# Layer 2's attention loop: sums and Newton step in other slots, values made four steps at a time

## The chip, the core and the metric

The kernel runs as one program on one core of a Trainium2 chip. The metric is device time in microseconds from start to end. The engines that matter here are TensorE (PE in the profile; its weight loads are PEld), VectorE (DVE), ScalarE (ACT), GpSimd (POOL) and the DMA queues. Each engine works through its own list of instructions in program order and waits on semaphores where it needs another's result. Matmul results go to PSUM[...].

## What is computed

The model is a chain of four cross-attention layers, each followed by a feed-forward layer, over 1024 tokens of width 128 and a context of 6404 rows. The change lies in the attention of layer 2. With 16 heads of width 8 its core is:

```python
qh = _split_heads(q @ Wq.T)
kh = _split_heads(k @ Wk.T)
vh = _split_heads(v @ Wv.T)
scores = jnp.einsum('bhqd,bhkd->bhqk', qh, kh) / jnp.sqrt(jnp.asarray(D, dtype=qh.dtype))
attn = jax.nn.softmax(scores, axis=1)
heads = jnp.einsum('bhqk,bhkd->bhqd', attn, vh)
return _merge_heads(heads) @ Wo.T
```

`q` is the normalized token matrix, `k` and `v` are both the context. The softmax runs over axis 1, the heads: for each pair of a token and a key, the 16 exponentials are divided by their own sum. So no sum over keys is needed, but every 128x512 block of scores needs a reciprocal of its own.

## The kernel before

`attn_heads` (L1268) works in steps. A step is one chunk of 128 keys (the 51st has 4) against one half of the tokens (512 columns): 51 chunks times two halves are 102 steps. A step has K = 8 slots; a slot handles two heads, so its tiles are [128 keys, 2 heads, 512 tokens]. From L1391 on the order of instructions on PE, ACT, DVE and POOL is the order written in the code (`manual_schedule`). One loop over slots (L1522 to L1549) writes it, with the parts of a step staggered over later slots. "Slot 0" to "slot 7" below mean the loop's `k`. In each slot it calls:

- `least_made` (L1348), ten slots ahead: two bf16 matmuls give approximate scores in the PSUM tile `pair_ps`, which has a single buffer; ScalarE copies them to `lb`. `least_so_far` (L1366), one slot later, folds them on VectorE into a running minimum (L1371; none in slot 7), and at a step's last pair into `mneg` (L1376). The minimum over heads keeps the exponentials in range.
- `exps` (L1431): four matmuls put the exact scores less the minimum into `x_ps` (two buffers), and ScalarE writes exponentials into `e` (L1445).
- `first_summed` (L1447), one slot later: a matmul with the identity adds one head into `s_ps` (one buffer), eight heads per step: those of pairs 0 to 3. So the first of a step, which stands in slot 1, writes into the buffer of the step before.
- `summed` (L1458), one slot later: VectorE adds pairs 4 to 7 with three additions of 128x1024 in slots 6, 7 and 0; also in slot 0 it adds the two halves of the result (L1470) and `s_ps` to it (L1471).
- `inverted` (L1475), in slot 1: the reciprocal of the sum, as Exp(-Ln) on ScalarE (L1480, L1481) and one Newton step on VectorE (L1482, L1483).
- `shared` (L1485), ten slots after `exps`: VectorE multiplies the pair by the reciprocal.
- `values` (L1492), thirteen slots after `exps`: matmuls of `e` with the values in `vz` collect in `o_ps`.
- `make_values` (L1417), once a step, in slot 5 and right ahead of the step's first `values`: a matmul (L1421) gives the values of 128 keys in `pair_ps`, and VectorE writes them, negated, into `vz` (L1425), in a layout with gaps: each head's 8 columns at the start of a 32-column group.

On PE the order in a slot is `least_made`, `exps`, `first_summed`, (`make_values`,) `values`. On VectorE it is (vz,) the minimum, the sums, the Newton step, the multiply. During the first steps the loop also makes the queries of the second half (`other`), and from step 55 on, in even slots, it takes pieces of the following feed-forward layer (`along`) until these are used up.

Of the kernel before, what the change touches and what calls it, by code (L numbers as in the profile page):

```python
# [10 lines left out]
F32 = mybir.dt.float32  # L11
# [4 lines left out]
AF = mybir.ActivationFunctionType  # L16
ALU = mybir.AluOpType
# [3 lines left out]
P = 128  # L21
S = 1024
NT = S // P
HALF = 512
HT = NT // 2
D = 128
# [18 lines left out]
class Net:  # L45
# [1222 lines left out]
    def attn_heads(self, ctxT, tiles, before, along):  # L1268
# [13 lines left out]
        nc, tc, a = self.nc, self.tc, self.a  # L1282
# [4 lines left out]
        K = NH // 2  # L1287
        scale = 8.0**-0.5
        with ExitStack() as st:
            kb, _, kst = tiles  # L1290
            big = st.enter_context(tc.tile_pool(name="a2big", bufs=1))
            qn = big.tile([P, 4, S], BF16, name="qn")
            qS = big.tile([P, 4, S], F32R, name="qS2")
            vz = [big.tile([P, 4 * 136], F32, name=f"vz{i}") for i in range(2)]
            wq = big.tile([P, D], F32, name="wq")
            wqs = big.tile([P, 4, D], F32, name="wqs")
            wv = big.tile([P, D], F32, name="wv")
# [42 lines left out]
            steps = [(c, at, n, half) for half in range(2) for c, (at, n) in enumerate(keys)]  # L1340
            N = len(steps)
            lows, mnegs, es, accs, sums, firsts, invs, kts, outs = ({} for _ in range(9))
# [5 lines left out]
            def least_made(slot):  # L1348

                i, k = divmod(slot, K)  # L1350
                c, at, n, half = steps[i]
                m = self.pair_tile()
                for t, (j, r) in enumerate(heads(k)):
                    nc.tensor.matmul(  # L1354
                        m[:n, t], kb[r, at : at + n], qn[r, j, ts(half, HALF)],
                        start=True, stop=True,
                    )
                if k == 0:
                    lows[i] = lp.tile([P, 2, HALF], BF16, tag="low", name="low")
                    t = lows[i]  # L1360
                else:
                    t = lp.tile([P, 2, HALF], BF16, tag="lb", name="lb", bufs=3)
                nc.scalar.copy(t[:n], m[:n])  # L1363
                return t
# [21 lines left out]
            pr = self.pool(st, "a2p", 2)  # L1386
# [11 lines left out]
            def exp_and_ln():  # L1398

                tc.keep_in_program_order(  # L1400
                    nc.scalar.preload_act_table_set("natural_log_exp_and_others")
                )

            def load_keys(i):
                _, at, n, _ = steps[i]
                kts[i] = pr.tile([P, 4, P], F32R, tag="kS", name="kS", bufs=3)
                if n < P:
                    nc.gpsimd.memset(kts[i].bitcast(F32), 0.0)
                for g in range(4):
                    nc.sync.dma_start(  # L1410
                        out=kts[i][32 * g : 32 * g + 32, :, :n].bitcast(F32),
                        in_=kst[P * g : P * g + P, at : at + n].rearrange(
                            "(j r) n -> r j n", j=4
                        ),
                    )

            def make_values(i):  # L1417

                _, at, n, _ = steps[i]
                m = self.pair_tile()  # L1420
                nc.tensor.matmul(m[:n, 0, :D], ctxT[:, at : at + n], wv, start=True, stop=True)  # L1421
                dst = vz[i % 2].rearrange("p (j x) -> p j x", x=136)[:n, :, :P]
                dst = dst.rearrange("p j (g y) -> p j g y", y=32)[:, :, :, :8]
                src = m[:n, 0, :D].rearrange("p (g j d) -> p j g d", g=4, j=4)
                nc.vector.tensor_scalar_mul(dst, src, -1.0)  # L1425

            def pair(i, k):
                at = 2 * (k % 2)
                return es[i, k // 2][: steps[i][2], at : at + 2]
# [16 lines left out]

            def first_summed(slot):  # L1447

                i, h = divmod(slot, K)
                if h == 0:  # L1450
                    firsts[i] = ps_s.tile([P, HALF], F32, tag="s", name="s_ps")
                n = steps[i][2]
                nc.tensor.matmul(  # L1453
                    firsts[i], self.ident[:n], es[i, h // 4][:n, h % 4],
                    start=h == 0, stop=h == K - 1,
                )

            def summed(slot):  # L1458
                i, k = divmod(slot, K)
                n = steps[i][2]  # L1460
                if k <= K // 2:
                    return
                if k == K // 2 + 1:
                    accs[i] = pr.tile([P, 2, HALF], F32, tag="acc", name="acc")
                acc = accs[i][:n]
                before = pair(i, k - 1) if k == K // 2 + 1 else acc
                nc.vector.tensor_tensor(acc, before, pair(i, k), ALU.add)
                if k == K - 1:
                    sums[i] = pr.tile([P, HALF], F32, tag="sum", name="sum")
                    nc.vector.tensor_tensor(sums[i][:n], acc[:, 0], acc[:, 1], ALU.add)  # L1470
                    nc.vector.tensor_tensor(  # L1471
                        sums[i][:n], firsts.pop(i)[:n], sums[i][:n], ALU.add
                    )

            def inverted(i):  # L1475

                n = steps[i][2]
                invs[i] = pr.tile([P, HALF], F32, tag="inv", name="inv")
                r, t, s = invs[i][:n], accs[i][:n, 0], sums[i][:n]
                nc.scalar.activation(t, s, AF.Ln)  # L1480
                nc.scalar.activation(r, t, AF.Exp, scale=-1.0)  # L1481
                nc.vector.tensor_tensor(t, s, r, ALU.mult)  # L1482
                nc.vector.scalar_tensor_tensor(r, t, 2.0, r, ALU.subtract, ALU.mult)  # L1483

# [7 lines left out]
            def values(i, j, part):  # L1492
                c, at, n, half = steps[i]
                if c == 0 and j == 0 and part == 0:
                    outs[half] = ps_o.tile([P, HALF], F32, tag="o", name="o_ps")
                for g in range(4):
                    cols = ts(part, HALF // 2)
                    nc.tensor.matmul(  # L1498
                        outs[half][32 * g : 32 * g + 32, cols],
                        vz[i % 2][:n, ds(P * j + 32 * g, 32)], es[i, j][:n, g, cols],  # L1500
                        start=c == 0 and j == 0 and part == 0,
                        stop=c == NK - 1 and j == 3 and part == 1,
                    )
                if c == NK - 1 and j == 3 and part == 1:
                    ob = lp.tile([P, HALF], F32, tag="q32", name="ob")
                    nc.scalar.copy(ob, outs[half])
                    y = self.m_tile()
                    for t in range(4):
                        nc.tensor.matmul(
                            y[:, ts(t, P)], ob[:, ts(t, P)], wo, start=True, stop=True  # L1510
                        )
                    self.add_to_tokens(y, half)

            SHARED = K + 2
            VALUES = K + 5
            SLOTS = N * K
            kept = {}
            other = make_queries(1)
# [3 lines left out]
            for slot in range(SLOTS + 3 * K):  # L1522
                i, k = divmod(slot, K)
                if k == 0 and i + 2 < N:
                    load_keys(i + 2)
                if slot + AHEAD < SLOTS:
                    kept[slot + AHEAD] = least_made(slot + AHEAD)
                if slot < SLOTS:
                    exps(slot)
                if 0 < slot <= SLOTS:  # L1530
                    first_summed(slot - 1)
                at = slot - VALUES
                if 0 <= at < SLOTS:
                    if at % K == 0:
                        make_values(at // K)
                    values(at // K, at % K // 2, at % 2)
                if slot - 1 + AHEAD in kept:
                    least_so_far(slot - 1 + AHEAD, kept.pop(slot - 1 + AHEAD))
                if 0 < slot <= SLOTS:
                    summed(slot - 1)  # L1540
                if 1 <= i <= N and k == 1:
                    inverted(i - 1)
                if 0 <= slot - SHARED < SLOTS:
                    shared(slot - SHARED)
                if 2 <= i < NK:
                    next(other, None)
                elif i >= NK + 4 and k % 2 == 0:
                    if next(along, None) == "other table":
                        exp_and_ln()  # L1549
# [414 lines left out]
```

## Time and profile before

| | us |
|---|---|
| median of 3 runs | 8147.5 (8136.12 to 8156.23) |
| the profiled execution: time | 8165.55 |
| the profiled execution: span of its instructions | 8163.5 |
| first to last start of L1445, layer 2's exponentials | 4231.0 to 6661.1 |

The granted TensorE clock is 0.959 of full speed over the whole span. Busy over the span are PE 7372.9 us (90%), DVE 6268.6 (77%) and ACT 4939.0 (61%).

Within layer 2's loop, by stretches of time (busy us of each engine, and the mean granted clock):

| stretch, us | what it holds | PE | DVE | ACT | clock |
|---|---|---|---|---|---|
| 4271 to 5377, 1105.5 us | steps of the first half | 995.8 | 972.4 | 811.4 | 0.99 |
| 5377 to 5464, 87.1 us | the chunk of 4 keys, change of halves | 80.1 | 61.3 | 51.2 | 0.78 |
| 5464 to 5534, 70.8 us | undisturbed | 62.0 | 63.8 | 50.0 | 1.00 |
| 5534 to 5885, 350.7 us | with pieces of the feed-forward layer | 297.7 | 316.9 | 233.0 | 0.94 |
| 5885 to 6622, 736.5 us | undisturbed | 669.9 | 643.0 | 537.5 | 0.97 |

How the lines in the next part are read. In the view of waits: who waited, for what, then the total in us, the number of times, and the longest. In the timeline: start in us, duration, engine, line, operation, out<-in, shapes, count, and in brackets the engine's idle time before it and what ended that. In the view of windows: the stretch, its length, the busy us of PE, PEld, DVE, ACT and POOL (instructions in brackets), the granted clock, the share of the DMA engines and GB/s. Consecutive VectorE operations overlap a little, so their starts lie closer than their durations: 1.13 to 1.14 us apart for 128x1024 fp32 (duration 1.22), 0.60 for the minimum (0.69).

### The profile page before, as it was taken

The page shows a single profiled execution, that of the slowest core. Times are in us where ns is not written, and L with a number is a line of the kernel's source. Part 1 is how long each engine was busy: PE and PEld are TensorE (multiplying, and loading weights), DVE is VectorE, ACT ScalarE, POOL GpSimd, SP SyncE. Part 2 cuts the span into 40 slices and gives each one's busy share as a digit, 9 for nine tenths or more (in the row PEclk, how much of TensorE's full clock was granted, in tenths as well). Part 3 has the DMA queues.
Part 4 walks back from the last instruction along what each step waited for, and adds up shares of the span by engine and source line. Part 5 has one row for each costly group of instructions (what it writes and reads, how often), then busy time and mean ns, then how long its engine had stood idle before and what let it go on. Part 6 is the DMA issues. An engine that isn't in the chain of part 4 may idle for free. (4 is left out here: it accounts for less than half of the span.)

```text
span 8163.5 us, 105249 instructions
## 1 busy us (share of the span) xinstructions
PE 7372.9 (90%) x41959; PEld 2806.6 (34%) x42169; DVE 6268.6 (77%) x7114; ACT 4939.0 (61%) x5829; POOL 1783.4 (22%) x1112
## 2 busy tenths in 40 slices
PE   6999999999999889999978999998899987999997
PEld 2333333333333433333343333332333323333334
DVE  6776777777775588888548888879888878888864
ACT  2444444444444467777757777766677746777765
POOL 4555555555556410000100000000000010000001
PEclk8999999999999899999989999999999978999988
DMA  1000000000000211010310000000000011100101
GB/s 29 1 2 2 1 2 1 2 2 1 1 1 1 73 28 16 11 19 11 112 37 11 12 12 13 12 10 11 11 12 12 12 45 32 19 11 13 17 5 39
DMA packets 145602, 134.96 MB, mean 17 GB/s; under 512 B 31530, under 2 KB 126054, under 8 KB 144206
## 3 DMA queue, kind: packets, MB, share of 16 engines
q1 hardware_dynamic: 134214, 104.37, 5.8%
q0 software_dynamic: 5936, 18.04, 0.7%
q8 instruction: 331, 5.42, 0.3%
q10 hardware_dynamic: 4960, 5.80, 0.2%
q14 instruction: 161, 1.32, 0.1%
HBM read 105.46 MB, written 35.85 MB: 17 GB/s over the span
## 5 line engine op out<-in xcount | busy, mean ns | idle before, releaser
L897 DVE TENSOR_REDUCE mx<-pair_ps 128x2 f32<-128x1024 f32 x1612 | 1811.3, 1178 | 253.8 <-PE pair_ps L893 229.8
L285 DVE TENSOR_REDUCE mx<-b_ps 128x2 f32<-128x1024 f32 x920 | 1091.5, 1186 | 639.5 <-PE b_ps L281 636.9
L331 ACT ACTIVATE pt<-x_ps,bias 128x1024 f32<-128x1024 f32 (+1 forms) x944 | 1000.9, 1110 | 877.6 <-PE x_ps L326 844.5
L345 POOL TENSOR_TENSOR acc<-acc,pt 128x1024 f32<-128x1024 f32 x544 | 1341.9, 2467 | 537.0 <-ACT pt L331 524.6
L1126 ACT ACTIVATE px<-x_ps 128x1024 f32<-128x1024 f32 x1088 | 1113.8, 1024 | 308.9 <-PE x_ps L1121 301.7
L1363 ACT CAST lb<-pair_ps 128x1024 bf16<-128x1024 f32 (+1 forms) x714 | 722.1, 1012 | 507.0 <-PE pair_ps L1354 494.6
L1453 PE MATMUL s_ps<-e,ident 128*128 128x512 f32 (+1 forms) x1632 | 877.7, 620 | 136.2 <-DVE sum L1471 134.8
L1490 DVE TENSOR_TENSOR e<-e,inv 128x1024 f32<-128x1024 f32 (+1 forms) x816 | 993.4, 1218 | 0.0
L351 PE MATMUL o_ps<-pt,v 128*64 128x512 f32 (+1 forms) x3776 | 915.9, 605 | 0.0
L1012 PE MATMUL o_ps<-px,v 128*32 128x512 f32 x4352 | 904.1, 620 | 0.0
L1012 PE MATMUL o_ps<-py,v 128*32 128x512 f32 x2176 | 896.7, 616 | 0.0
L326 PE MATMUL x_ps<-q,kT 64*128 64x512 f32 (+1 forms) x3776 | 894.8, 592 | 0.0
L893 PE MATMUL pair_ps<-kb,qz 64*128 64x512 bf16 (+1 forms) x3224 | 827.8, 386 | 59.8 <-DVE mx L897 33.7
L1445 ACT ACTIVATE e<-x_ps 128x1024 f32<-128x1024 f32 (+1 forms) x816 | 841.0, 1031 | 34.6 <-PE x_ps L1442 34.6
L1126 ACT ACTIVATE py<-y_ps 128x512 f32<-128x512 f32 x1088 | 647.7, 595 | 323.8 <-PE y_ps L1121 322.9
L1121 PE MATMUL x_ps<-qS,kS 33*128 33x512 f32 x2176 | 711.7, 531 | 127.9 <-ACT px L1126 127.9
L345 DVE TENSOR_TENSOR acc<-acc,pt 128x1024 f32<-128x1024 f32 (+1 forms) x368 | 629.6, 1711 | 66.2 <-ACT pt L331 66.1
L1498 PE MATMUL o_ps<-e,vz 128*32 128x256 f32 (+1 forms) x6528 | 546.6, 407 | 57.3 <-DVE vz L1425 53.2
L1121 PE MATMUL y_ps<-qS,kS 33*128 33x512 f32 x1088 | 567.4, 522 | 4.3 <-ACT py L1126 4.3
L1371 DVE TENSOR_TENSOR low<-lb,low 128x1024 bf16<-128x1024 bf16 (+1 forms) x714 | 488.4, 684 | 8.7 <-ACT lb L1363 8.5
L1438 PE MATMUL x_ps<-qS,kS 32*128 32x512 f32 x1632 | 487.8, 593 | 0.0
L1442 PE MATMUL x_ps<-mneg,identb 128*128 128x512 bf16 x1422 | 454.9, 390 | 34.5 <-issue 34.5
(374 smaller groups left out, 8010.2 us busy)
## 6 DMA issues: line engine op xcount, KB each, us to landing
kS<-kst SPq DMA_DIRECT2D x400, 64.0 KB
kS<-kd SPq DMA_DIRECT2D x112, 200.1 KB
w<-in_L_ffn_w SPq DMA_DIRECT2D x48, 256.0 KB
kst<-kd POOLq DMA_DIRECT2D x24, 512.0 KB, 13.7
kd<-kh SPq DMA_DIRECT2D x12, 512.0 KB
kd<-k SPq DMA_DIRECT2D x12, 512.0 KB
qS<-qd SPq DMA_DIRECT2D x256, 16.0 KB
kb<-in_L_ffn_w SPq DMA_DIRECT2D x16, 256.0 KB
```

Source lines behind the costliest of these rows:

```text
L285: nc.vector.tensor_reduce(mxs[u][:, t, :, b], m[:, :, :n], AX.X, ALU.max)
L326: nc.tensor.matmul(s[:n, g], kT[p % 2][r, at : at + n], qs[p][r, ts(half, HALF)], start=False, stop=True,)
L331: nc.scalar.activation(pt[:n], s[:n], AF.Exp, bias=bias[:n, c : c + 1])
L345: eng.tensor_tensor(acc[:n], acc[:n], pt[:n], ALU.add)
L351: nc.tensor.matmul(o[cols], v[:n, c, cols], pt[:n, g], start=c == 0, stop=c == NKT - 1)
L897: nc.vector.tensor_reduce(mxs[u][:, t, b], m[:, :, :n], AX.X, ALU.max)
L1012: nc.tensor.matmul(o[32 * j : 32 * j + 32], v[:, c, ds(VW * h, 32)], pt, start=i == 0, stop=c + 2 >= NK,)
L1121: nc.tensor.matmul(s[:, k], kS[p % 2][r, ts(c, P)], qS[u % 2][r], start=True, stop=True,)
L1126: nc.scalar.activation(pt[:, : len(some)], s[:, : len(some)], AF.Exp)
L1445: nc.scalar.activation(pair(i, k), s[:n], AF.Exp)
L1453: nc.tensor.matmul(firsts[i], self.ident[:n], es[i, h // 4][:n, h % 4], start=h == 0, stop=h == K - 1,)
L1490: nc.vector.tensor_tensor(e, e, r, ALU.mult)
```

## The change

`make_values` now makes the values of four steps with four matmuls into one half of a pair tile, and ScalarE copies them, negated, into a new buffer `v4` with one activation (or one per step where a chunk is short). A new `spread_values`, once a step, lays out one step's part of `v4` into `vz` on ScalarE. `first_summed` takes heads 0 to 5 and 10, 11 (pairs 0, 1, 2 and 5); VectorE adds pairs 3, 4, 6 and 7, in slots 5, 7 and 0, and the two 128x512 additions come in slot 1 of the next step. `inverted` keeps Ln and Exp, now in slot 2; the Newton step becomes `improved`, in slot 3. The multiply comes eleven slots after `exps` instead of ten, the value matmuls fourteen instead of thirteen. `spread_values` is called two slots ahead of a step's first value matmul, in slot 4; `make_values` five slots ahead, in slot 1 of every fourth step, behind the value matmuls of its slot on PE.

```diff
+            v4 = big.tile([P, 4, D], F32, name="v4")
...
             def make_values(i):
...
-                _, at, n, _ = steps[i]
-                m = self.pair_tile()
-                nc.tensor.matmul(m[:n, 0, :D], ctxT[:, at : at + n], wv, start=True, stop=True)
+                four = steps[i : i + 4]
+                m = self.pair_tile()[:, 0].rearrange("p (s d) -> p s d", d=D)
+                for s, (_, at, n, _) in enumerate(four):
+                    nc.tensor.matmul(
+                        m[:n, s], ctxT[:, at : at + n], wv, start=True, stop=True
+                    )
+                full = [n == P for _, _, n, _ in four]
+                if all(full):
+                    nc.scalar.activation(v4[:, : len(four)], m[:, : len(four)], AF.Copy, scale=-1.0)
+                    return
+                for s, (_, at, n, _) in enumerate(four):
+                    nc.scalar.activation(v4[:n, s], m[:n, s], AF.Copy, scale=-1.0)
+
+            def spread_values(i):
+                n = steps[i][2]
                 dst = vz[i % 2].rearrange("p (j x) -> p j x", x=136)[:n, :, :P]
                 dst = dst.rearrange("p j (g y) -> p j g y", y=32)[:, :, :, :8]
-                src = m[:n, 0, :D].rearrange("p (g j d) -> p j g d", g=4, j=4)
-                nc.vector.tensor_scalar_mul(dst, src, -1.0)
+                nc.scalar.copy(dst, v4[:n, i % 4].rearrange("p (g j d) -> p j g d", g=4, j=4))
...
             def first_summed(slot):
...
-                i, h = divmod(slot, K)
-                if h == 0:
+                i, k = divmod(slot, K)
+                if k == 0:
                     firsts[i] = ps_s.tile([P, HALF], F32, tag="s", name="s_ps")
                 n = steps[i][2]
+                h = k if k < 6 else k + 4
...
             def summed(slot):
+
                 i, k = divmod(slot, K)
+                if k == 0:
+                    i -= 1
+                if i < 0:
+                    return
                 n = steps[i][2]
-                if k <= K // 2:
-                    return
-                if k == K // 2 + 1:
+                if k == 4:
                     accs[i] = pr.tile([P, 2, HALF], F32, tag="acc", name="acc")
-                acc = accs[i][:n]
-                before = pair(i, k - 1) if k == K // 2 + 1 else acc
-                nc.vector.tensor_tensor(acc, before, pair(i, k), ALU.add)
-                if k == K - 1:
-                    sums[i] = pr.tile([P, HALF], F32, tag="sum", name="sum")
+                    nc.vector.tensor_tensor(accs[i][:n], pair(i, 3), pair(i, 4), ALU.add)
+                elif k in (6, 7):
+                    acc = accs[i][:n]
+                    nc.vector.tensor_tensor(acc, acc, pair(i, k), ALU.add)
+                elif k == 0:
+                    acc = accs[i][:n]
+                    sums[i] = pr.tile([P, HALF], F32, tag="sum", name="sum", bufs=1)
                     nc.vector.tensor_tensor(sums[i][:n], acc[:, 0], acc[:, 1], ALU.add)
...
                 nc.scalar.activation(t, s, AF.Ln)
                 nc.scalar.activation(r, t, AF.Exp, scale=-1.0)
+
+            def improved(i):
+                n = steps[i][2]
+                r, t, s = invs[i][:n], accs[i][:n, 0], sums[i][:n]
                 nc.vector.tensor_tensor(t, s, r, ALU.mult)
                 nc.vector.scalar_tensor_tensor(r, t, 2.0, r, ALU.subtract, ALU.mult)
...
-            SHARED = K + 2
-            VALUES = K + 5
+            SHARED = K + 3
+            VALUES = K + 6
...
                 if 0 <= at < SLOTS:
-                    if at % K == 0:
-                        make_values(at // K)
                     values(at // K, at % K // 2, at % 2)
+                if 0 <= at + 2 < SLOTS and (at + 2) % K == 0:
+                    spread_values((at + 2) // K)
+                if 0 <= at + 5 < SLOTS and (at + 5) % (4 * K) == 0:
+                    make_values((at + 5) // K)
...
-                if 0 < slot <= SLOTS:
+                if 0 < slot <= SLOTS + 1:
                     summed(slot - 1)
-                if 1 <= i <= N and k == 1:
+                if 1 <= i <= N and k == 2:
                     inverted(i - 1)
+                if 1 <= i <= N and k == 3:
+                    improved(i - 1)
```

More of the change, by code (lines that the diff above doesn't have):

```diff
@@ L1447, in first_summed @@
             def first_summed(slot):
-                i, h = divmod(slot, K)
-                if h == 0:
+                i, k = divmod(slot, K)
+                if k == 0:
                     firsts[i] = ps_s.tile([P, HALF], F32, tag="s", name="s_ps")
                 n = steps[i][2]
+                h = k if k < 6 else k + 4
                 nc.tensor.matmul(
                     firsts[i], self.ident[:n], es[i, h // 4][:n, h % 4],
-                    start=h == 0, stop=h == K - 1,
+                    start=k == 0, stop=k == K - 1,
                 )
```

## The prediction

> **What bounds the kernel now.** The change touches one stage, so I first asked the page where that stage lies: the exponentials of L1445 run from 4231.0 to 6661.1 us and the value matmuls of L1498 end at 6681, about 2.45 ms of a span of 8163.5. In the busy times of that stretch PE (TensorE) stands at about 90% and DVE (VectorE) at 87%: shares that do not say which of them sets the pace. The starts of the value matmul L1421, one per step, do: among the undisturbed steps 22.46 us is by far the commonest distance.
>
> Next, who waits for whom from 4350 to 5370 us, 45 steps without other work:
>
> ```profile
> DVE vz L1425 <- PE pair_ps L1421: 106.6, 45, 3.7
> PEld s_ps L1453 <- ACT e L1445: 86.1, 44, 2.2
> PE s_ps L1453 <- DVE sum L1471: 66.3, 45, 1.8
> ```
>
> PE waits for VectorE once a step (1.47 us on average), and VectorE for PE once a step (2.4 us). Each holds the other up: a loop, not one full engine. The timeline around the first wait, at full clock:
>
> ```profile
> 5066.23 0.39 PE L1354 MATMUL pair_ps<-qn,kb 32*128 32x512 bf16 x2
> ...
> 5067.17 0.69 DVE L1470 TENSOR_TENSOR sum<-acc 128x512 f32<-128x512 f32 x1
> ...
> 5067.96 0.69 DVE L1471 TENSOR_TENSOR sum<-s_ps,sum 128x512 f32<-128x512 f32 x1
> ...
> 5068.80 1.10 PE L1453 MATMUL s_ps<-e,ident 128*128 128x512 f32 x2 [1.41 <-DVE sum L1471]
> ...
> 5070.40 0.39 PE L1354 MATMUL pair_ps<-qn,kb 32*128 32x512 bf16 x2
> ...
> 5071.39 1.02 PE L1453 MATMUL s_ps<-e,ident 128*128 128x512 f32 x2
> ...
> 5072.92 0.39 PE L1354 MATMUL pair_ps<-qn,kb 32*128 32x512 bf16 x2
> ```
>
> The reader is to see that a slot without a wait takes PE 2.52 us (5070.40 to 5072.92), its sum matmul starting 0.99 after the slot does, and that this one takes 4.17: s_ps has one buffer, and the first sum matmul of a step needs L1471 of the step before. The other wait, in VectorE's timeline one step earlier and later:
>
> ```profile
> 5057.77 0.29 DVE L1425 TENSOR_SCALAR vz<-pair_ps 128x128 f32<-128x128 f32 x1 [2.17 <-PE pair_ps L1421]
> ...
> 5080.23 0.29 DVE L1425 TENSOR_SCALAR vz<-pair_ps 128x128 f32<-128x128 f32 x1 [2.16 <-PE pair_ps L1421]
> ```
>
> Now the loop closes. From the end of L1471 (5068.65): 0.15 to PE's restart, 1.60 to the next slot, three slots 7.56, 2.27 to the vz copy, and from a vz copy to the next end of L1471 10.88 (5057.77 to 5068.65). Sum **22.46**, the measured step. In PE's ledger: 8 x 2.52 = 20.16, 0.67 at the values (such a slot takes 3.19) and 1.63 at the sum.
>
> The clock matters too. After the longer idle at 5021 the granted clock (third column from the right) falls to half:
>
> ```profile
> 5022.00:5023.00 1.00, 0.64 (x2) 0.30 (x2) 1.00 (x2) 0.72 (x2) 0.00 (x0) 0.93 0.03 8
> 5023.00:5024.00 1.00, 1.00 (x6) 0.17 (x8) 1.00 (x3) 0.54 (x1) 0.00 (x0) 0.50 0.00 0
> 5026.00:5027.00 1.00, 0.79 (x3) 0.42 (x2) 1.00 (x3) 0.84 (x2) 0.00 (x0) 0.86 0.00 0
> ```
>
> It lasts some 3.4 us and makes the step 24.03 instead of 22.46, so 1.57 dearer. Of 68 undisturbed steps with a gap of 1.40, 13 show it; of 11 with a gap of 1.75 (a pause of VectorE of 0.46 ahead of L1471, every fourth step of the first half), 5.
>
> **The change, part by part.** *The vz copy leaves VectorE* (102 x 0.29 = 30 us). Its own time is hidden; what goes is its wait, and with it PE's 0.67 per step, 68 us in all. ScalarE gets 102 strided 128x128 copies: no row shows the form; the nearest are 372 ns (a 128x128 activation, L635) and 249 ns (a 4x128 copy, L268). I take 0.37, 38 us if nothing hid it, in slot 4, where ScalarE idles 0.58 before the next lb. The Trainium skill (ScalarE: Activation LUTs, Rules for kernel authors) speaks against it: multiplies belong on VectorE. By that rule the move loses 0.08 per step; by the row it takes away a wait of 2.16. Neither 0.29 nor 0.37 is on the path, so the row of the wait decides.
>
> *Values of four steps at once.* 26 blocks. Four matmuls of the same shape take 1.16 (L1509 at 5459.89), 0.04 to ScalarE, 0.60 for its 128x512 copy (597 ns, L1324), 0.05 to the matmul of the next slot that needs the single pair buffer: 1.85, some 0.05 of it under the matmuls before: **1.8**. Behind that pair matmul waits all of PE. Bounds: 1.4, if weight loads hide and the matmuls run in 0.8; 2.7 at half clock, where the four take 2.07. The block stands in slot 1, right after the stalled sum, so it lies on the loop: 26 x 1.8 = 47 us, 0.45 per step.
>
> *Which pairs the two engines sum* (0, 1, 2 and 5 on PE; 3, 4, 6 and 7 on VectorE): counts equal, no cost.
>
> *The sums move from slot 0 to slot 1, the Newton step to slot 3, Ln and Exp to slot 2.* This decides. L1471 now stands in the very slot whose sum matmul waits for it, where before it stood one slot ahead; and Newton can begin only when ScalarE has done slot 2's exponential, Ln and Exp. Round the new loop, from the end of the sum: 0.15 and 1.60 to PE's slot 2; 1.34 to its exponential (5070.40 to 5071.74); 0.94 to Ln (1.03 less the usual overlap); 0.66 to Exp (5068.69 to 5069.35); 0.66 to Newton (5716.58 to 5717.24): 5.35. Then VectorE until the next sum ends, no wait on the way: two Newton operations, each waiting for its forerunner, 2 x 0.72 = 1.44; nine 128x1024 operations (six multiplies, three adds) at their spacing of 1.135, 10.22; five minima at 0.60, 3.00; mneg 0.12 + 0.34; L1470 to L1471 0.79; L1471 0.69: 16.60. Loop **21.95**. VectorE's idle moves to before Newton: its two multiplies and two minima after the sum end at 3.39, Newton comes at 5.35, so it waits 1.96 there instead of 2.16 before vz. Queued behind Newton are the multiplies that the value matmuls need, but three slots ahead of use. Ln and Exp in slot 2 make ScalarE 0.6 late in slot 3; its 0.48 of slack per slot absorbs that.
>
> PE's wait does not go: slot 1 begins at 1.75 + 7 x 2.52 = 19.39 and restarts at 22.10, 2.71 later against 2.57 before. The gap grows from 1.41 to 1.55.
>
> **Sum.** Three steps of 21.95 and one of 23.75: mean 22.40 against 22.46, -0.06 x 102 = **-6 us**. Falls of the clock: 19% at 1.40 and 45% at 1.75 give about 30% at 1.55; 79 undisturbed steps x 0.30 = 24 against 18, 6 x 1.57 = **+9 us**. Here the skill's rule (TensorE: Matmul & The Clock Gate, HAM oscillation) is that idle gaps above about 3.4 us re-throttle; by it neither kernel falls and the sum is -6; by the rows it is +3. I follow the rows. The 13 steps that carry the next layer's quantization (5534 to 5885, 27.0 each, VectorE busy 24.4): its operations come at the end of even slots. Before, those of slots 0, 2 and 4 lay between the sum and the vz copy, where VectorE waited; in the new loop only slot 2's fall into a wait. About 4.3 per step are added (24.4 less 20.1 in quiet steps); three quarters of it on the new loop make 21.95 + 3.2 = 25.2, 0.8 above VectorE's own total: 13 x 0.8 = 10 us lost at worst, against 0.67 per step won at the values, 9. I take 0, within 10.
>
> Together +3 us. On the profiled run (8165.55 us, span 8163.5, 18 above the median of the three runs) that is 8169; on the median 8147.5, **8150**.
>
> **Rivals.**
> - *No measurable change, as summed*: 0.52. Own range 8125 to 8172.
> - *Slower: a clock fall with every block.* PE idles 1.55 at the sum, works 2.7, then idles 0.65 for ScalarE's copy. If each of some 20 undisturbed blocks brings a fall besides 30% of the other 59 steps, that is 38 falls, 14 more than I count: +22; if the matmuls then run at half clock, a block costs 2.7 instead of 1.8: 20 x 0.9 = +18. 8150 + 40 = 8190. It decides once about 14 falls come on top. For it: falls grow with the gap; against: the second gap alone is below any that a fall followed. 0.31.
> - *Faster: the wait at the sum shrinks to nothing*, PE's 20.16 + 0.45 = 20.6 per step; 1.8 x 79 = 142 us: 8005. It is what dealing the sums evenly would give if VectorE could run ahead (its 20.0 per step would fit); against it stands the loop, which needs no full engine. 0.05. A milder form: a step of 22.40 whose rhythm avoids falls saves 6 + 18 x 1.57 = 34: 8114. 0.12.
>
> The change does what it says: the sums are dealt; only the wait they feed is not.
>
> **Numbers.** About 0.3% (24 us) is what a measurement of this kernel can tell from no change. Faster 0.05 + 0.12 = 0.17; within 0.52; slower 0.31. The range 8105 to 8205 takes in the milder gain and the slower rival with its dearer blocks and leaves out the large gain.
>
> **What would show it.** In the new trace: no wait before a vz write; VectorE idle about 2 us before the Newton multiply in each step; PE still idle 1.5 to 1.6 at the first sum matmul; distances between those of 21.95, 21.95, 21.95 and 23.75 at full clock; the clock at half after about 24 of the undisturbed steps. Wrong it would be if PE's gap at the sum were under 1 us (the loop does not hold), if a block cost above 2.3, or if half clock followed most steps.

## The result, and the profile after

The changed kernel takes 8188.2 us (median of four runs, 8180.6 to 8195.6) against 8142.1 (8136.1 to 8156.2), four runs as well. The recorded ratio, which is not the quotient of the two medians, is 1.0051, with an interval of 1.0038 to 1.0063. It is 46 us slower, inside the stated range, but not the "no measurable change" held likeliest, whose own range ended at 8172. The profiled execution has a span of 8178.9 us.

The undisturbed steps did what the sum said. Here is the view of waits of the changed kernel over the same stretch as before, 4350 to 5370 us (who waited, for what, total us, times, longest; a selection):

```profile
PE s_ps L1466 <- DVE sum L1489: 68.3, 44, 1.6
DVE acc L1504 <- ACT inv L1499: 64.5, 45, 1.7
ACT v L1428 <- PE pair_ps L1423: 40.4, 11, 4.7
PE pair_ps L1355 <- ACT v L1428: 7.5, 11, 0.7
```

The wait before vz is gone. PE's wait at the sum is not (1.55 us each time), and VectorE's wait now stands before the Newton step. The timeline of one such step, slots 1 to 3, shows both:

```profile
5122.77 0.39 PE L1355 MATMUL pair_ps<-qn,kb 32*128 32x512 bf16 x2
...
5124.65 0.69 DVE L1489 TENSOR_TENSOR sum<-s_ps,sum 128x512 f32<-128x512 f32 x1
...
5125.49 1.10 PE L1466 MATMUL s_ps<-e,ident 128*128 128x512 f32 x2 [1.56 <-DVE sum L1489]
...
5127.09 0.39 PE L1355 MATMUL pair_ps<-qn,kb 32*128 32x512 bf16 x2
...
5128.56 0.69 DVE L1372 TENSOR_TENSOR low<-lb,low 128x1024 bf16<-128x1024 bf16 x1 [0.35 <-ACT lb L1364]
...
5130.66 0.69 DVE L1504 TENSOR_TENSOR acc<-sum,inv 128x512 f32<-128x512 f32 x1 [1.41 <-ACT inv L1499]
```

PE starts its slot 1 at 5122.77, and its sum matmul 2.72 later, because L1489 ends only at 5125.34. VectorE idles 0.35 and 1.41 before Newton. Some distances between steps (starts of mneg, L1376 before and L1377 after, steps 30 to 33) are:

```
before  22.46  22.45  22.47  24.35
after   23.32  21.95  23.79  21.95
```

21.95 is the step at full clock, 23.79 one with a block of values, 23.32 and 24.35 steps with the clock at half. Over 78 undisturbed steps the mean is 22.85 before and 22.80 after.

The time went where the loop carries pieces of the feed-forward layer: the 13 steps from the 55th on take 352.5 us before and 378.4 after. The waits of PE for VectorE's sum and vz copy in the stretch from 5534 to 5885 us, first of the kernel before:

```profile
PE o_ps L1498 <- DVE vz L1425: 17.8, 13, 3.4
...
PE s_ps L1453 <- DVE sum L1471: 12.4, 6, 2.6
```

and of the changed kernel, where no wait for vz is left:

```profile
PE s_ps L1466 <- DVE sum L1489: 59.4, 12, 8.1
```

Counted over the same 13 steps of both, PE waits 48 us more at the sum (60.3 against 12.4) and 18 less at vz. Its idle time of all kinds grows from 55.6 to 78.4 us, its busy time only from 296.9 to 300.1.

How a piece does that is seen in the changed kernel's timeline, slots 0 and 1 of one of these steps:

```profile
5821.82 1.22 DVE L1512 TENSOR_TENSOR e<-e,inv 128x1024 f32<-128x1024 f32 x1
5822.96 0.68 DVE L1606 TENSOR_REDUCE sc<-h 128x32 f32<-128x512 f32 x1
...
5825.55 0.35 DVE L1619 RECIPROCAL tmp<-tmp 128x32 f32<-128x32 f32 x1
5825.82 0.63 DVE L1372 TENSOR_TENSOR low<-lb,low 128x1024 bf16<-128x1024 bf16 x1
5826.37 0.68 DVE L1488 TENSOR_TENSOR sum<-acc 128x512 f32<-128x512 f32 x1
5827.15 0.69 DVE L1489 TENSOR_TENSOR sum<-s_ps,sum 128x512 f32<-128x512 f32 x1
5827.76 1.22 DVE L1512 TENSOR_TENSOR e<-e,inv 128x1024 f32<-128x1024 f32 x1
5827.99 2.05 PE L1466 MATMUL s_ps<-e,ident 128*128 128x512 f32 x2 [3.84 <-DVE sum L1489]
```

Ten small operations of a piece, 2.86 us from 5822.96 to 5825.82, are queued at the end of slot 0, so the sums of slot 1 stand behind them, and PE behind the sums: 3.84 us idle, where a quiet step has 1.56. Pieces of slots 4 and 6 that have made VectorE late act in the same way; in these 13 steps the wait at the sum lies between 0.9 and 8.1 us. In the kernel before, the sums came first in slot 0 and the piece after them. The matmul itself then takes 2.05 instead of 1.10, as the windows explain (third column from the right, the granted clock):

```profile
5827.00:5828.00 1.00, 0.01 (x1) 0.04 (x1) 0.90 (x3) 0.00 (x0) 0.00 (x0) 0.85 0.00 0
5828.00:5829.00 1.00, 1.00 (x2) 0.46 (x2) 1.00 (x2) 0.00 (x0) 0.00 (x0) 0.50 0.00 0
```

In the two profiled executions the loop is 28.8 us longer after (2398.5 against 2369.7 from its first mneg to its last): 26 more in the steps with pieces and 7 more in the loop's first three, 3 less in the quiet steps and about 1 less elsewhere. Outside the loop, where nothing changed, the two differ by 13 the other way. So one pair of profiles does not say whether the pieces are all of the 46 us of the medians; that was left to experiments.

### The profile page after: what moved, and what is told of

The parts are those of the page before. It is cut to its first block, busy times and chain, and to the rows that moved or that the text cites. A ratio compares the mean times of both kernels' runs of the same rounds, so it can differ in the third digit from the quotient of the medians.

```text
span 8178.9 us, 105096 instructions
## 1 busy us (share of the span) xinstructions
PE 7363.4 (90%) x41961; PEld 2790.0 (34%) x42169; DVE 6250.8 (76%) x7012; ACT 4951.7 (61%) x5961; POOL 1784.9 (22%) x1112
```

## Experiments

The kernels were timed in three groups, each with the kernel before beside them, and each ratio is to that one. Its medians were 8148 (the three kernels that take the change apart, and pieces in slots 1 and 2), 8144 (the moves of the sums, and pieces behind the loop) and 8154 (the others).

**Values alone, sums alone, and the sums moved back.** The change joins two independent parts. Three kernels take it apart. The first keeps the values and puts the two short additions, Ln and Exp back where they were:

```diff
-                if k == 0:
-                    i -= 1
-                if i < 0:
-                    return
                 n = steps[i][2]
...
-                elif k == 0:
+                if k == K - 1:
                     acc = accs[i][:n]
...
-                if 0 < slot <= SLOTS + 1:
+                if 0 < slot <= SLOTS:
                     summed(slot - 1)
-                if 1 <= i <= N and k == 2:
+                if 1 <= i <= N and k == 1:
                     inverted(i - 1)
```

> The changed kernel with the two 128x512 additions back in slot 0 (right behind the last 128x1024 addition), Ln and Exp back in slot 1, the Newton step left in slot 3, values made as in the change. Loop theory: the sum no longer stands in the slot whose matmul waits for it, and Newton no longer waits for ScalarE, so no loop is longer than PE's own work: steps of 20.2 with one of 22.0 in four, mean 20.6 instead of 22.4, no clock fall at the sum; 79 x 1.8 + 24 x 1.57 = 180 us less than the changed kernel, some 8010. Rival (the blocks of four steps and the clock falls behind them carry the loss): the blocks are still there, so at most the 30 us of the sums' part come back, 8155 or more.

Measured: 7966.1, a ratio of 0.9769 (0.9749 to 0.9789) to the kernel before. Steps run 20.14, 21.57, 20.54, 20.13, mean 20.6. From 4400 to 5200 us PE waits for no sum; among the waits between engines that are left are these:

```profile
ACT lb L1364 <- PE pair_ps L1355: 104.9, 194, 0.6
ACT v L1428 <- PE pair_ps L1423: 13.5, 10, 1.4
DVE low L1372 <- ACT lb L1364: 13.2, 10, 1.3
PE pair_ps L1355 <- ACT v L1428: 6.9, 10, 0.7
```

Of 78 undisturbed steps none shows a fall of the clock. The loop theory's step is met; the rival, blocks and clock falls behind them, is out: the blocks are still there. The median lies 44 us below the expected 8010. In the profiles the loop is 211 us shorter than the changed kernel's: 171 in the quiet steps, where 180 were expected, and 19 in the steps with pieces and 21 in its other steps, which the expectation had left out.

The second is the kernel before with only the values made and laid out as in the change (`make_values`, `spread_values` and their calls, as in the diff of the change):

```diff
-                    sums[i] = pr.tile([P, HALF], F32, tag="sum", name="sum")
+                    sums[i] = pr.tile([P, HALF], F32, tag="sum", name="sum", bufs=1)
...
-                    if at % K == 0:
-                        make_values(at // K)
                     values(at // K, at % K // 2, at % 2)
+                if 0 <= at + 2 < SLOTS and (at + 2) % K == 0:
+                    spread_values((at + 2) // K)
+                if 0 <= at + 5 < SLOTS and (at + 5) % (4 * K) == 0:
+                    make_values((at + 5) // K)
```

> The kernel before with only the values part of the change: four steps' values at once, copied and laid out by ScalarE; sums, Ln, Exp and Newton where they were (sum has one buffer instead of two, to make room). Loop theory: the loop ran through the vz copy; without it PE's wait at the sum falls from 1.6 to about 0.9 in most steps, mean step 21.1 with the block, few clock falls: 79 x 1.3 + 28 = 130 us less than before, some 8010 to 8030. Rival: the blocks cost as much as they save or more: 8140 or above.

Measured: 7995.9, ratio 0.9811 (0.9794 to 0.9828), steps of 21.1 on average as expected, the median 14 us below the expected range. So this part gains 152 us by itself.

The third is the changed kernel with the values as before (the same lines taken back, in the kernel after):

```diff
+                    if at % K == 0:
+                        make_values(at // K)
                     values(at // K, at % K // 2, at % 2)
-                if 0 <= at + 2 < SLOTS and (at + 2) % K == 0:
-                    spread_values((at + 2) // K)
-                if 0 <= at + 5 < SLOTS and (at + 5) % (4 * K) == 0:
-                    make_values((at + 5) // K)
```

> The changed kernel with the values made as before (once a step, copied by VectorE into vz ahead of the value matmuls), sums, Ln, Exp and Newton as in the change. Loop theory: the sum loop of 21.95 plus PE's 0.67 at the values, about 22.65 per step, gaps of about 1.6 to 1.75 at the sum with clock falls in 35 to 45% of the quiet steps: 20 to 70 us slower than the kernel before, 8160 to 8210. Rival (the blocks carry the loss): without blocks it is no slower than the kernel before, 8140 or less.

Measured: 8364.0, ratio 1.0261 (1.0243 to 1.0279): the direction of the loop theory, but far beyond its number. Its step at full clock is 23.71 instead of 22.65. VectorE's timeline tells what was missed:

```profile
5008.08 1.22 DVE L1500 TENSOR_TENSOR e<-e,inv 128x1024 f32<-128x1024 f32 x1
5010.78 0.29 DVE L1425 TENSOR_SCALAR vz<-pair_ps 128x128 f32<-128x128 f32 x1 [1.48 <-PE pair_ps L1421]
5010.99 0.68 DVE L1371 TENSOR_TENSOR low<-lb,low 128x1024 bf16<-128x1024 bf16 x1
```

The vz copy lies between Newton and the sum, that is on the new loop, with its wait of 1.48 and 0.21 more: 21.95 + 1.69 = 23.64. I had added PE's delay, not VectorE's. PE's gap at the sum, expected at 1.6 to 1.75, grows with it to 2.66 (4350 to 5370 us):

```profile
PE s_ps L1454 <- DVE sum L1477: 111.7, 42, 2.7
```

At this gap 38 of 76 undisturbed steps fall to half clock, 19 of them for 6.8 us instead of 3.4.

The four kernels together: neither 8148, values 7996, sums 8364, both 8188. The values gain 152 to 176, the sums lose 192 to 216, and what the change shows is the difference of two large numbers.

**Which move of the sums costs.** Two kernels undo one each: the short additions back in slot 0 with Ln and Exp left in slot 2 (the diff of the first kernel without its last pair of lines), and the reverse (that pair alone).

> The changed kernel with only the two 128x512 additions back in slot 0; Ln and Exp stay in slot 2, Newton in slot 3. If the sum standing in the slot of the waiting matmul is what costs: nearly all of the gain of the kernel with both moved back (7966) is here, steps of some 20.3 and 22, 7970 to 8000. If the late inverse (Ln and Exp in slot 2, Newton waiting for them) costs by itself: half or less of the gain, 8060 or above.

Measured: 7980.2, ratio 0.9802 (0.9787 to 0.9817), steps of 20.33 and 22.17.

> The changed kernel with only Ln and Exp moved back to slot 1 (behind the sum, which stays in slot 1); Newton stays in slot 3. If the late inverse costs by itself, the loop is broken and steps fall to about 20.6 on average: below 8030. If the same-slot sum costs: PE still waits about 1.1 to 1.3 us in slot 1, steps of about 21.5 and 23.3, fewer clock falls: 8100 to 8140.

Measured: 8109.3, ratio 0.9957 (0.9943 to 0.9970), steps of 21.45 and 23.43. PE still waits at the sum, here from 4350 to 5370 us:

```profile
PE s_ps L1466 <- DVE sum L1489: 48.5, 46, 1.1
```

So the sum in the slot of the matmul that waits for it costs 143 us with the early inverse (8109 against 7966) and 208 with the late one (8188 against 7980). The late inverse costs 79 where the sum is in slot 1 (8188 against 8109), and 14 where it is in slot 0 (7980 against 7966). Each makes the other dearer, as two stretches of one loop would. Part of the 79 is the clock: at the gap of 1.07 the quiet steps show no fall, and 20 falls of some 1.5 us, as the changed kernel has them, are about 30 us by estimate.

**Quiet steps or steps with pieces.** Both kernels were run with every piece taken behind the loop, by `done(along)`:

```diff
-                elif i >= NK + 4 and k % 2 == 0:
+                elif i >= NK + 4 and False:
```

> The changed kernel with all feed-forward pieces of the first half taken behind the loop, none in it. To be read against the kernel before with the same move. If the change's loss lies in the steps with pieces: the two differ by no more than 15 us. If it lies in the quiet steps: by 30 to 50 us.

> The kernel before with all feed-forward pieces of the first half taken behind the loop. The base for the changed kernel with the same move: within 15 us of it if the loss lies in the steps with pieces, 30 to 50 us faster than it if the loss lies in the quiet steps. In itself some 54 us less in the loop than before, and the pieces' own time behind it.

Measured: 8210.1 (8197.8 to 8213.8) with the change and 8208.3 (8202.4 to 8212.0) without. Without pieces in it the change leaves the loop as it was, 2313.2 us against 2315.0 without the change in their profiles. The loss of 46 us needs the pieces.

**The place of the pieces.** Three kernels halve their rate to two slots a step, over some 27 steps: the changed kernel with slots 1 and 2, which lie in VectorE's wait for the inverse; the same with slots 0 and 6, ahead of the sum; and the kernel before with slots 2 and 4, ahead of the vz copy.

```diff
-                elif i >= NK + 4 and k % 2 == 0:
+                elif i >= NK + 4 and k in (1, 2):
```

> The changed kernel with the feed-forward pieces taken in slots 1 and 2 only (two a step instead of four, so over some 27 steps instead of 13). If the pieces of slots 0, 4 and 6, which lie ahead of the sum on VectorE, carry the loss: they now fall into VectorE's wait for the inverse and 15 to 35 us of the loss come back, 8150 to 8172. If the loss lies in the quiet steps: no change within 8 us of the changed kernel's 8188.

Measured: 8153.9, ratio 1.0009 (1.0000 to 1.0018): 34 us of the 46 come back, 40 when each kernel is set against the kernel before of its own group. The wait at the sum, from 5500 to 6200 us:

```profile
PE s_ps L1466 <- DVE sum L1489: 51.9, 26, 5.3
```

> The changed kernel with the feed-forward pieces in slots 0 and 6 only: the same halved rate as with slots 1 and 2 (8154), but both slots ahead of the sum on VectorE. If the place of the pieces counts: clearly slower than 8154, 8180 or above. If the halved rate alone brought the gain: 8154 within 10.

Measured: 8200.2, ratio 1.0053 (1.0039 to 1.0067). The same wait over the same stretch:

```profile
PE s_ps L1466 <- DVE sum L1489: 84.2, 25, 6.6
```

Same rate, same pieces, other slots: 46 us by the medians, 41 against the kernel before of each group. So it is not the halved rate that brought the gain.

> The kernel before with its pieces in slots 2 and 4 only, both between the sum and the vz copy, where VectorE waits: the same halving and sheltering for the old loop. If sheltered pieces cost the old loop little in any case: 8115 to 8140, still some 20 to 30 us faster than the changed kernel with sheltered pieces (8154) or equal to it; the more equal, the more the pieces are the whole difference.

Measured: 8149.0, ratio 0.9995 (0.9987 to 1.0003). The expected 8115 to 8140 is missed: it is equal to the kernel before, and within 5 us of the changed kernel with sheltered pieces. The old loop had sheltered three of its four slots already.

**A version that beats the kernel before and the changed one.** The first kernel (sums in slot 0, Ln and Exp in slot 1, Newton in slot 3, values in blocks) with its pieces in slots 2 and 6:

```diff
-                elif i >= NK + 4 and k % 2 == 0:
+                elif i >= NK + 4 and k in (2, 6):
```

> The kernel with sums in slot 0, Ln and Exp in slot 1, Newton in slot 3 and the values in blocks (7966), with the pieces in slots 2 and 6 instead of every even slot. VectorE is nearly full in each step (20.0 of 20.6), so halving the rate spreads about 54 us of extra work over twice the steps and lets 0.6 us per step absorb some: 7940 to 7965. If VectorE's total decides alone: no change.

Measured: 7953.8 (7942.7 to 7964.0), ratio 0.9752 (0.9737 to 0.9767): 200 us below the kernel before. That it beats the first kernel too is not shown: its median is 12 us lower, but in another group, and the intervals of the two ratios overlap.

## Why the prediction was right and wrong

*In part luck: the range.* The measured 8188 lies in 8105 to 8205 because the range took in the slower rival with its 8190. That rival's mechanism did not happen, and the sum's own 8150, with 8125 to 8172, is missed.

*Right: the loop.* The step at full clock was summed to 21.95 and is 21.95; with a block 23.75 against 23.79, so the block costs 1.84 instead of 1.8. PE's gap at the sum is 1.56 against 1.55. VectorE's wait before Newton was put at 1.96 in one piece and comes as 0.35 and 1.41. ScalarE's strided copy, bounded by rows of 249 and 372 ns and taken as 370, is 299, and the profile shows no engine that waits for it.

*Right: the clock.* 24 falls in 79 quiet steps were expected from the share of falls at gaps of 1.40 and 1.75; there are 20 in 78, against 17 before. The choice of the trace's rows over the rule of the Trainium skill (TensorE: Matmul & The Clock Gate, HAM oscillation), gaps above about 3.4 us, stands: all these gaps are far shorter. That the count came near is luck in part, since the length of the gap alone does not decide (last section). The sum for quiet steps, +3 us, fits two medians 2 us apart with no pieces in the loop.

*Wrong: the steps with pieces.* "I take 0, within 10" is the term that failed; it is 26 us in the one pair of profiles and 44 between the medians (46 with pieces, 2 without). Where the other 18 lie is not shown. The working saw that the pieces of slots 0, 4 and 6 would lie on the new loop, and put three quarters of 4.3 us, 3.2 a step, on it. PE's wait at the sum grew by about that: 4.6 us a step against 1.56 in quiet steps. What failed is what it was set against: VectorE's own total of 24.4 a step, a pace that the kernel before, with its 27.0, did not keep. So 3.2 a step were booked as 0.8. In the old loop one quarter of the pieces, those of slot 6, lay on the loop: 1.1 a step. The same rule for both loops gives 2.1 a step, 28 us in 13 steps; this estimate is made afterwards, and the trace has 26. The 9 us set against the loss, PE's 0.67 at the values, had also been spent once: the quiet steps' sum of -0.06 a step ran over all 102. Two finer points were not in the working. A piece is not spread but keeps VectorE for 0.3 to 3.3 us in one slot, and none of the 13 steps gives anything back: each is longer than its counterpart before, by 0.3 to 5.8 us. And 11 of these 13 waits at the sum are followed by a fall of the clock, which stands at 0.90 over the stretch, 0.94 before; as PE is busy only 3 us longer, little of the 26 is seen to come from that.

*The rivals.* The slower one named the right side for the wrong reason: 7 of the 20 falls come in steps with a block, 13 of the 20 blocks in quiet steps bring none, and the 7 falls begin at the wait for the sum, ahead of the block's own gap. The large gain was dismissed because the loop stood against it, and that was right for this change. The number worked out for it, 20.6 a step, is what the first experiment measured once the loop was cut: it could have been read as the price of the sums' place.

## What to carry to other kernels

An operation that another engine waits for belongs as early as its inputs allow, not where the queue looks emptiest: here, dealing work evenly over slots put the sum into the very slot whose matmul needed it, and cost more than the 152 us that the other part gained. Follow each wait round until it closes on itself, and add up every duration on the way; here that sum, and not the busiest engine, was the step, and what was queued on that way, such as pieces of another layer, lengthened it. And measure the parts of a change apart: a result near zero can be a large gain and a large loss.

## What the hardware showed

In quiet steps the granted clock falls to half for about 3.4 us after gaps of 1.4 to 1.8 us in PE's work, in some steps and not in others: 17 of 78 before, 20 of 78 after, where most gaps are of 1.56. It does so in 38 of 76 at the gap of 2.66 in the kernel with the sums alone. It never does in the 75 quiet steps with a gap of 1.07 in the kernel that moves back Ln and Exp only, nor in the 78 of the kernel without a wait at the sum. Each fall of 3.4 us costs 1.4 to 1.6 us in this loop.

The traces also show which gaps bring a fall. Within the loop the starts of the half-clock stretches fit a grid of 3.413 us to within 1 ns, in the profile before and in the one after. Before, 12 of 67 quiet gaps of 1.40 us are followed by a fall. Those 12 ended 0.06 to 0.31 us ahead of a point of the grid; none of the other 55 ended there. After, the 17 falls behind gaps of 1.54 to 1.58 us begin between 0.12 us before the gap's end and 0.55 behind it. So where a gap ends in this rhythm counts as well as how long it is. What the chip measures over that period was not tried.
